# A two-layer graph network on one core: where the output blocks of step 2 get their two layer normalizations

## The chip, the core and the metric

The kernel runs on one core of a Trainium2 chip. The core has five engines with instruction queues of their own: TensorE (PE) for matrix products, VectorE (DVE), ScalarE (ACT), GpSimd (POOL), and SyncE (SP), which here issues most of the DMAs. Each engine works through its queue in order and waits at an instruction until what it needs is there. The metric is the time of one launch on the device, in microseconds; lower is better.

## The reference, cut to what matters

Two layers on 2708 nodes with 256 features. Layer 0 is `x1 = layernorm(x + relu([x, adj @ x] @ W + b))`. Layer 1, on `X = x1`, with `S = adj`:

```
R  = (S + I) / rowsum(S + I)
Xf = Xa = X;  Z = 0
for n in (0, 1):                        # "step 1" and "step 2"
    A  = top_p_attention(Xa)            # softmax, largest entries up to a mass of 0.9, renormalized
    Xf = R @ Xf
    Xa = A @ Xa
    Z  = Z + Xf @ U1[n].T + Xa @ U2[n].T
h   = X + Z
out1 = (h - mean(h)) / sqrt(var(h) + 1e-5) * ln_g + ln_b
out = layernorm(X + out1)
```

The last two lines are what the change is about. For each of the 22 blocks of 128 rows, a block `h` is normalized, multiplied by `g`, added to `x1 + b` (a copy of which lies in HBM as `x1b`), normalized again, and written out.

## The kernel before

All rows are cut into 22 blocks of 128 (the last has 20). Step 2 is a loop over 23 periods (line 1059), and each period over six slots `g` (line 1070). The instructions of all engines are issued in the order in which the Python loop names them; there is no planner, so the order written there is the order in every engine's queue. In period `per`:

- VectorE finds the exact top-p set of block `per`: `last_level` (926 to 930) and `finish2` (934), a generator that is advanced once per slot: line 942 over the whole row, 20 maxima (945), an ordering of 48 candidates (546, 548), small work (955 to 973), five match-replaces (976), of which three come in slot 4 and two in slot 5, and last line 979 over the whole row, which leaves the masked weights.
- TensorE and ScalarE multiply block `per - 1` with `ya`: in each slot `turn` (507) transposes four 128 x 128 pieces on TensorE and ScalarE copies them out of PSUM (516); `products` (522) multiplies the pieces of the slot before. The first transposes of a period need line 979 of the period before.
- ScalarE computes exponentials of block `per + 2` (`exps2`, 785) from logits that TensorE leaves in PSUM, and two trials of a threshold for block `per + 1` (`try_act`, 884, lines 889 and 892 over the whole row). The logits' PSUM tile `lg` is there only once.
- `shift` (781) computes two biases on VectorE: `nmax`, and `half` from it (783).
- `r_units` (687) multiplies gathered columns of `adj` with gathered rows of `yf` or `v`, eight products for each block. GpSimd gathers those rows by indirect DMAs (667), seven for a block, into `yg`, which has room for two blocks; a gather waits until TensorE has used what lay there.
- A block has its `h` when both its product with `R` and its product with the attention weights have arrived (`arrive`, 730, line 737); it is then put in `ready`. `base`, what line 737 adds to, is loaded by SyncE (716).

The finals: `final_slot` (1024) is called once per slot. It takes up to two blocks from `ready` in a period and drives each through its stages in a fixed slot: slot 2 loads `x1b` (996), slot 3 computes mean and variance on VectorE (1001, 1003), slot 4 takes the square root on ScalarE (1008) and then runs `middle` on VectorE (1012 to 1016), which subtracts, multiplies by `g`, scales, adds `x1b`, and computes the second statistics; slot 5 takes the second root; slot 0 of the next period runs `end`, the second normalization on VectorE (145, 146) into a buffer `o`, and the output DMA (1022). `c.gb[:, 0, :]` is `g`.

The buffers: `yg` (477) lies in a room with tag `Y`, used before by the transposed input, and does not fill it. The attention product of step 1 uses the line numbers from 829 to 878; lines 603 (VectorE over the whole row) and 362 (a GpSimd sum of 128 x 128) belong to that step.

Of the kernel before, what the change touches and what calls it, by code (L numbers as in the profile page):

```python
# [133 lines left out]
def ln_stats(nc, small, eps, h, p):  # L134
    st = small.tile([P, 6], FP, tag="bst", name="bst")
    nc.vector.bn_stats(st[:p], h[:p])
    mv = small.tile([P, 2], FP, tag="bmv", name="bmv", bufs=6)
    nc.vector.bn_aggr(mv[:p], st[:p])
    sd = small.tile([P, 1], FP, tag="bsd", name="bsd", bufs=6)
    nc.scalar.activation(sd[:p], mv[:p, 1:2], AF.Sqrt, bias=eps[:p], scale=1.0)  # L140
    return mv, sd
# [7 lines left out]
def fast_path(ctx, tc, c, flags, fint, xT_d, x_d, w0_d, b0_d, w1_d, w2_d, w3_d, u1_d, u2_d, g_d, b_d):  # L149
# [327 lines left out]
    yg = big.tile([P, 2, CC + 1, D], FP, tag="Y", name="yg")  # L477
# [279 lines left out]
    nc.gpsimd.memset(halfn, N / 2)  # L757
    ranks = small.tile([P, 8], FP, tag="ranks", name="ranks", bufs=1)
# [226 lines left out]
    finals = []  # L985

    class Final:
# [10 lines left out]
        def stats(self):  # L998
            p = self.p
            st = small.tile([P, 6], FP, tag="bst", name="bst")  # L1000
            nc.vector.bn_stats(st[:p], self.h[:p])
            self.mv = small.tile([P, 2], FP, tag="bmv", name="bmv", bufs=6)
            nc.vector.bn_aggr(self.mv[:p], st[:p])

        def root(self):
            p = self.p
            self.sd = small.tile([P, 1], FP, tag="bsd", name="bsd", bufs=6)
            nc.scalar.activation(self.sd[:p], self.mv[:p, 1:2], AF.Sqrt, bias=c.eps[:p], scale=1.0)

        def middle(self):  # L1010
            h, p, x1b, sd, mv = self.h, self.p, self.x1, self.sd, self.mv
            nc.vector.reciprocal(sd[:p], sd[:p])
            nc.vector.scalar_tensor_tensor(h[:p], h[:p], mv[:p, 0:1], c.gb[:p, 0, :],
                                           op0=ALU.subtract, op1=ALU.mult)
            nc.vector.scalar_tensor_tensor(h[:p], h[:p], sd[:p], x1b[:p], op0=ALU.mult, op1=ALU.add)
            self.stats()

        def end(self):
            t, p = self.t, self.p
            o = work.tile([P, D], FP, tag="mid", name="o")  # L1020
            ln_apply(nc, o[:p], self.h, p, self.mv, self.sd)
            nc.sync.dma_start(out=out_d[t * P:t * P + p, :], in_=o[:p])

    def final_slot(i):

        if i == 2:
            while ready and len(finals) < 2:
                finals.append(Final(*ready.pop(0)))
        stages = {2: ["load"], 3: ["stats"], 4: ["root", "middle"], 5: ["root"], 0: ["end"]}
        for n in stages.get(i, []):  # L1030
            for f in finals:
                getattr(f, n)()
        if i == 0:
            finals.clear()
# [24 lines left out]
    for per in range(NB + 1):  # L1059
# [10 lines left out]
        for g in range(NG):  # L1070
# [22 lines left out]
            if g == 0:  # L1093
# [4 lines left out]
                final_slot(0)  # L1098
# [11 lines left out]
            if g:  # L1110
                final_slot(g)

# [382 lines left out]
```

## Time and profile before

| what | value |
|---|---|
| time, median of 3 runs | 1440.12 us (1436.54 to 1440.23) |
| span of the profiled run | 1436.7 us |
| TensorE, VectorE, ScalarE, GpSimd busy | 91%, 75%, 51%, 39% |
| step 2's loop over periods | from about 800 us to 1420 us |
| line 1008, table loads for the square root | 8, of 1283 ns |
| line 1013, 1015 on VectorE | 22 each, 466 and 485 ns |
| line 146 on VectorE, into `o` | 22, 412 ns |
| line 362 on GpSimd, 128 x 128 | 22, median 499 ns, longest 3268 ns |
| line 667 on GpSimd, gathers | 308, median 946 ns |

An instruction's row in a timeline gives its start and duration in microseconds, the engine, the line, the operation, what it writes and reads (`out<-in`), the shapes, and in brackets how long the engine sat idle before it and for what. The shares of the first rows are means over stages that have quite different limits: TensorE is busy nearly all of the time in layer 0 and step 1, and less so in the second half of step 2. So the rows for single periods, which the prediction shows, say more about this change.

### The profile page before, as it was taken

How to read it: one execution, taken by the hardware profiler on the slowest of the kernel's cores; microseconds unless marked ns; L12 is line 12 of the kernel's file. 1: busy time of each engine (PE TensorE's matmuls, PEld its weight loads, DVE VectorE, ACT ScalarE, POOL GpSimd, SP SyncE). 2: the span in 40 equal slices, each digit the busy share in tenths (PEclk: the TensorE clock that was granted, in tenths of full speed). 3: DMA queues.
4: the chain of work that ended last, by engine and by line, in shares of the span. 5: the costliest groups of instructions: out<-in, count | busy, mean ns of one | idle time of the engine just before them, and what ended most of it. 6: DMA issues, size and time to landing. Idle time of an engine off the chain costs nothing.

```text
span 1436.7 us, 19034 instructions
## 1 busy us (share of the span) xinstructions
PE 1302.2 (91%) x5788; PEld 913.3 (64%) x5788; DVE 1078.2 (75%) x3665; ACT 729.7 (51%) x1316; POOL 559.1 (39%) x552
## 2 busy tenths in 40 slices
PE   5999999989899999999999699999979887888874
PEld 4778777833566666666664477676657565565652
DVE  1455555865988877777740899999999989898995
ACT  1100001025555555555553588787878776677721
POOL 1000000003454424775552787766247444334410
PEclk8999999999999999999998899999999889788886
DMA  7345444412131110322132546454425433334430
GB/s 205 124 152 159 150 141 148 156 49 68 64 95 64 63 36 20 97 93 69 63 69 66 176 138 189 130 171 127 104 89 163 127 121 121 111 110 132 123 89 24
DMA packets 92832, 157.96 MB, mean 110 GB/s; under 512 B 16356, under 2 KB 65196, under 8 KB 92720
## 3 DMA queue, kind: packets, MB, share of 16 engines
q1 hardware_dynamic: 66434, 100.59, 21.7%
q0 software_dynamic: 20544, 51.17, 12.9%
q10 hardware_dynamic: 5742, 4.89, 1.3%
q8 instruction: 48, 0.79, 0.2%
q14 instruction: 64, 0.52, 0.1%
HBM read 125.33 MB, written 31.26 MB: 109 GB/s over the span
## 4 chain that ended last, share of the span: by engine, by line
PE 54%; DVE 30%; ACT 11%; DMA 2%; issue 2%; SPq 0%; ACTq 0%; DVEq 0%
PE acc L533 16%; PE acc L250 14%; PE lg L493 6%; PE tr L513 5%; DVE e L979 4%; DVE w L976 4%; DVE cand L945 4%; PE misc L646 3%; DVE w L942 3%; ACT w L892 3%; DVE spare L548 2%; ACT w L889 2%; DVE srt L546 2%; PE acc L618 2%; PE misc L420 2%
## 5 line engine op out<-in xcount | busy, mean ns | idle before, releaser
L516 ACT COPY wT<-tr 128x512 f32<-128x512 f32 (+2 forms) x264 | 134.1, 512 | 271.9 <-PE tr L513 269.6
L533 PE MATMUL acc<-ya,wT 128*128 128x256 f32 (+1 forms) x924 | 239.2, 399 | 2.9 <-ACT wT L516 2.9
L667 POOL DMA_INDIRECT yg<-v_d,ix x154 | 153.9, 999 | 197.9 <-PE misc L699 130.8
L533 PE MATMUL acc<-x,wT 128*128 128x256 f32 (+1 forms) x924 | 230.5, 388 | 0.0
L513 PE MATMUL tr<-ident,e 128*128 128x128 f32 (+1 forms) x968 | 160.9, 288 | 73.0 <-DVE bulk L980 70.5
L667 POOL DMA_INDIRECT yg<-yf_d,ix x154 | 181.8, 1181 | 93.0 <-PE misc L699 55.0
L533 PEld LDWEIGHTS acc<-x,wT 128*128 128x128 f32 (+1 forms) x924 | 165.2, 189 | 79.5 <-issue 46.9
L533 PEld LDWEIGHTS acc<-ya,wT 128*128 128x128 f32 (+1 forms) x924 | 175.7, 198 | 56.1 <-issue 22.3
L250 PE MATMUL acc<-y,adj_t 128*128 128x257 f32 (+1 forms) x924 | 208.8, 382 | 0.0
L513 PEld LDWEIGHTS tr<-ident,e 128*128 128x128 f32 (+1 forms) x968 | 121.5, 148 | 123.9 <-issue 97.3
L699 PE MATMUL misc<-yg,adj_t 128*128 128x256 f32 (+1 forms) x660 | 186.3, 418 | 9.1 <-DVE v L722 5.2
L250 PEld LDWEIGHTS acc<-y,adj_t 128*128 128x128 f32 (+1 forms) x924 | 171.5, 189 | 34.0 <-issue 10.3
L360 POOL DMA_INDIRECT adj_t<-in_adj,ix x154 | 169.5, 1101 | 51.0 <-issue 39.3
L699 PEld LDWEIGHTS misc<-yg,adj_t 128*128 128x128 f32 (+1 forms) x660 | 125.1, 204 | 59.0 <-issue 17.7
L493 PE MATMUL lg<-k,q 64*128 64x512 f32 (+3 forms) x528 | 153.5, 610 | 6.7 <-ACT e L789 4.8
L539 DVE MAX8 cand<-e 128x8 f32<-128x170 f32 (+1 forms) x352 | 88.2, 319 | 42.5 <-ACT e L500 42.5
L327 POOL DMA_DIRECT2D part_d<-e x1 | 0.6, 573 | 306.3 <-DVE e L326 306.3
L889 ACT ACTIVATE w<-e,st 128x2708 f32<-128x2708 f32 (+1 forms) x43 | 113.7, 2645 | 0.0
L892 ACT ACTIVATE w<-e,st 128x2708 f32<-128x2708 f32 (+1 forms) x42 | 111.2, 2647 | 0.1
L431 ACT COPY x1T<-tr 128x256 f32<-128x256 f32 (+1 forms) x22 | 8.0, 364 | 192.2 <-PE tr L430 182.8
L945 DVE MAX8 cand<-w 128x8 f32<-128x136 f32 (+1 forms) x440 | 94.4, 285 | 0.8
L546 DVE MAX8 srt<-spare 128x8 f32<-128x128 f32 (+3 forms) x264 | 81.4, 308 | 9.1
(218 smaller groups left out, 1787.5 us busy)
## 6 DMA issues: line engine op xcount, KB each, us to landing
adj_t<-in_adj SPq DMA_DIRECT2D x44, 704.0 KB
adj_t<-adjc_d SPq DMA_DIRECT2D x44, 448.0 KB
adjc_d<-adj_t SPq DMA_DIRECT2D x22, 256.0 KB
base<-za_d SPq DMA_DIRECT2D x41, 128.0 KB
adjc_d<-adj_t SPq DMA_DIRECT2D x22, 192.0 KB
xt<-in_x ACTq DMA_DIRECT2D x21, 128.0 KB
x_d<-x SPq DMA_DIRECT2D x21, 128.0 KB
x1b_d<-xb SPq DMA_DIRECT2D x21, 128.0 KB
```

Of the source, the lines that this page charges most:

```text
L250: nc.tensor.matmul(acc[:p, :n], lhsT=halves[k // KH][:kw, k % KH, :p], rhs=y[:kw, k, :n], start=k == 0, stop=stop and k == NB - 1)
L360: nc.gpsimd.indirect_dma_start(out=a[:CW, i, :], out_offset=None, in_=adj_rows, in_offset=bass.IndirectOffsetOnAxis(ap=ix[:CW, m, i:i + 1] ...
L493: nc.tensor.matmul(lg[:p, h, :b - a], lhsT=q[o, t * P:t * P + p], rhs=keys[s][o, i, :b - a], start=True, stop=True)
L513: nc.tensor.transpose(tr[:kw, k % 4, :p], e[:p, k * P:k * P + kw], ident[:p, :p])
L516: nc.scalar.copy(wT[:, :full, :p], tr[:, :full, :p])
L533: nc.tensor.matmul(acc[:p, :D], lhsT=wT[:kw, k % 4, :p], rhs=y[:kw, k, :], start=k == 0, stop=k == NB - 1)
L546: nc.vector.max(dst[:p, i:i + 8], src[:p])
L667: nc.gpsimd.indirect_dma_start(out=y[:CW, i, :], out_offset=None, in_=rows_d, in_offset=bass.IndirectOffsetOnAxis(ap=ix[:CW, m, i:i + 1], ...
L699: nc.tensor.matmul(acc[:p, :D], lhsT=a[:kw, k, :p], rhs=rhs, start=k == 0, stop=k == CC)
L889: nc.scalar.activation(scr[:b.p, :N], e, AF.Relu, bias=b.nz, scale=b.l[k], accum_out=b.relu)
L892: nc.scalar.activation(scr[:b.p, :N], e, AF.Sign, bias=b.nz, scale=b.l[k], accum_out=b.sign)
L945: nc.vector.max(cand[:p, 8 * i:8 * i + 8], w[:p, SEG2 * i:SEG2 * (i + 1)])
```

## The change

It gives the finals of step 2 another division of labour and another rhythm.

- Normalizing is now `h * (1/sd) + (-mean/sd)`. VectorE computes the two numbers per row (a reciprocal and a product of one column), ScalarE does the 256 columns by an `Identity` activation with a scale and a bias per row. This holds for both normalizations.
- Between them, the product with `g` and the sum with `x1b` go to GpSimd.
- A block's finals are stretched over two periods: in slot 3 it is loaded, in slot 4 first statistics and root, in slot 5 `middle`; in the next period, second statistics and root in slot 4, `end` in slot 5. So in slots 4 and 5 two new blocks (`new`) and two older ones (`finals`) are treated together.
- Since `h` lives longer, the first normalization writes into one of four spare buffers, cut from the unused end of the room with tag `Y`; the second works in place, and the output DMA reads from there. `mv` and `sd` get 8 buffers in place of 6.
- After the last period (`tail`), what is left is done on VectorE as before.
- Apart from that, `half` in `shift` moves from VectorE to ScalarE, between the two exponentials that frame it.

It is meant to take elementwise work from VectorE, and to take the square root out of the middle of VectorE's queue.

```diff
-    yg = big.tile([P, 2, CC + 1, D], FP, tag="Y", name="yg")
+    y_room = big.tile([P, DC * N], FP, tag="Y", name="yg")
+    YW = 2 * (CC + 1) * D
+    yg = y_room[:, :YW].rearrange("p (s c d) -> p s c d", s=2, d=D)
+    spares = [y_room[:, YW + D * i:YW + D * (i + 1)] for i in range(4)]
...
     def shift(b, lg):
         nc.vector.tensor_reduce(b.nmax, lg[:, :P], AX.X, ALU.max, negate=True)
-        nc.vector.tensor_scalar(b.half, b.nmax, 0.5, math.log(F * GUESS ** 0.5), op0=ALU.mult, op1=ALU.add)
...
         if i == 0:
+            nc.scalar.activation(b.half, b.nmax, AF.Identity, bias=part_of[:b.p], scale=0.5)
             nc.scalar.activation(e2(b.t)[:b.p, HC:2 * HC], lg, AF.Exp, bias=b.half, scale=0.5, accum_out=b.roots)
...
+        def norm(self, dst):
+            p, h, mv, sd = self.p, self.h, self.mv, self.sd
+            nc.vector.reciprocal(sd[:p], sd[:p])
+            nc.vector.tensor_scalar(mv[:p, 1:2], mv[:p, 0:1], sd[:p], -1.0, op0=ALU.mult, op1=ALU.mult)
+            if tail:
+                nc.vector.tensor_scalar(h[:p], h[:p], sd[:p], mv[:p, 1:2], op0=ALU.mult, op1=ALU.add)
+            else:
+                nc.scalar.activation(dst[:p], h[:p], AF.Identity, bias=mv[:p, 1:2], scale=sd[:p])
+                self.h = dst
...
         def middle(self):
-            nc.vector.reciprocal(sd[:p], sd[:p])
-            nc.vector.scalar_tensor_tensor(h[:p], h[:p], mv[:p, 0:1], c.gb[:p, 0, :],
-                                           op0=ALU.subtract, op1=ALU.mult)
-            nc.vector.scalar_tensor_tensor(h[:p], h[:p], sd[:p], x1b[:p], op0=ALU.mult, op1=ALU.add)
-            self.stats()
+            if tail:
...
+            spares.append(spares.pop(0))
+            self.norm(spares[-1])
+            h = self.h
+            nc.gpsimd.tensor_tensor(h[:p], h[:p], c.gb[:p, 0, :], op=ALU.mult)
+            nc.gpsimd.tensor_tensor(h[:p], h[:p], self.x1[:p], op=ALU.add)
 
         def end(self):
-            o = work.tile([P, D], FP, tag="mid", name="o")
-            ln_apply(nc, o[:p], self.h, p, self.mv, self.sd)
-            nc.sync.dma_start(out=out_d[t * P:t * P + p, :], in_=o[:p])
+            self.norm(self.h)
+            nc.sync.dma_start(out=out_d[t * P:t * P + p, :], in_=self.h[:p])
 
     def final_slot(i):
-        if i == 2:
-            while ready and len(finals) < 2:
-                finals.append(Final(*ready.pop(0)))
-        stages = {2: ["load"], 3: ["stats"], 4: ["root", "middle"], 5: ["root"], 0: ["end"]}
...
+        if i == 3:
+            while ready and len(new) < 2:
+                new.append(Final(*ready.pop(0)))
+                new[-1].load()
+        if i == 4:
+            for f in new + finals:
+                f.stats()
+            for f in new + finals:
+                f.root()
+        if i == 5:
+            for f in finals:
+                f.end()
+            for f in new:
+                f.middle()
+            finals[:] = new
+            new.clear()
...
-                final_slot(0)
...
+    tail.append(True)
...
-    final_slot(0)
     arrive(t, base, accs.pop(t), ras.pop(t)[:rows(t)])
     while ready or finals:
-        for g in (2, 3, 4, 5, 0):
+        for g in (3, 4, 5):
             final_slot(g)
```

More of the change, by code (lines that the diff above doesn't have):

```diff
@@ L136, in ln_stats @@
     nc.vector.bn_stats(st[:p], h[:p])
-    mv = small.tile([P, 2], FP, tag="bmv", name="bmv", bufs=6)
+    mv = small.tile([P, 2], FP, tag="bmv", name="bmv", bufs=8)
     nc.vector.bn_aggr(mv[:p], st[:p])
-    sd = small.tile([P, 1], FP, tag="bsd", name="bsd", bufs=6)
+    sd = small.tile([P, 1], FP, tag="bsd", name="bsd", bufs=8)
     nc.scalar.activation(sd[:p], mv[:p, 1:2], AF.Sqrt, bias=eps[:p], scale=1.0)
@@ L757, in fast_path @@
     nc.gpsimd.memset(halfn, N / 2)
+    part_of = small.tile([P, 1], FP, tag="part_of", name="part_of", bufs=1)
+    nc.gpsimd.memset(part_of, math.log(F * GUESS ** 0.5))
     ranks = small.tile([P, 8], FP, tag="ranks", name="ranks", bufs=1)
@@ L983, in finish2 @@
         ras[t] = ra
-    finals = []
+    new, finals = [], []
+    tail = []
     class Final:
@@ L1001, in stats @@
             nc.vector.bn_stats(st[:p], self.h[:p])
-            self.mv = small.tile([P, 2], FP, tag="bmv", name="bmv", bufs=6)
+            self.mv = small.tile([P, 2], FP, tag="bmv", name="bmv", bufs=8)
             nc.vector.bn_aggr(self.mv[:p], st[:p])
@@ L1006, in root @@
             p = self.p
-            self.sd = small.tile([P, 1], FP, tag="bsd", name="bsd", bufs=6)
+            self.sd = small.tile([P, 1], FP, tag="bsd", name="bsd", bufs=8)
             nc.scalar.activation(self.sd[:p], self.mv[:p, 1:2], AF.Sqrt, bias=c.eps[:p], scale=1.0)
-        def middle(self):
-            h, p, x1b, sd, mv = self.h, self.p, self.x1, self.sd, self.mv
-            nc.vector.reciprocal(sd[:p], sd[:p])
-            nc.vector.scalar_tensor_tensor(h[:p], h[:p], mv[:p, 0:1], c.gb[:p, 0, :],
-                                           op0=ALU.subtract, op1=ALU.mult)
-            nc.vector.scalar_tensor_tensor(h[:p], h[:p], sd[:p], x1b[:p], op0=ALU.mult, op1=ALU.add)
-            self.stats()
+        def norm(self, dst):
[7 more added lines that the diff above has]
+                self.h = dst
@@ new lines, in middle @@
+        def middle(self):
+            p = self.p
+            if tail:
+                h = self.h
+                mv, sd = self.mv, self.sd
+                nc.vector.reciprocal(sd[:p], sd[:p])
+                nc.vector.scalar_tensor_tensor(h[:p], h[:p], mv[:p, 0:1], c.gb[:p, 0, :],
+                                               op0=ALU.subtract, op1=ALU.mult)
+                nc.vector.scalar_tensor_tensor(h[:p], h[:p], sd[:p], self.x1[:p], op0=ALU.mult, op1=ALU.add)
+                return
+            spares.append(spares.pop(0))
+            self.norm(spares[-1])
+            h = self.h
+            nc.gpsimd.tensor_tensor(h[:p], h[:p], c.gb[:p, 0, :], op=ALU.mult)
+            nc.gpsimd.tensor_tensor(h[:p], h[:p], self.x1[:p], op=ALU.add)
@@ L1029, in final_slot @@
-        stages = {2: ["load"], 3: ["stats"], 4: ["root", "middle"], 5: ["root"], 0: ["end"]}
-        for n in stages.get(i, []):
-            for f in finals:
-                getattr(f, n)()
-        if i == 0:
-            finals.clear()
+        if i == 3:
[7 more added lines that the diff above has]
+                f.root()
```

## The prediction, made before the changed kernel was run

> **What bounds the kernel now.** I first read the slices of the page: in the last third VectorE stands at 9 in almost every slice, TensorE at 7 or 8, so TensorE waits for somebody. The chain of waits then splits the loop over the periods: VectorE rows carry it up to 1075 us, after that ScalarE rows appear between VectorE's. Next, the table by stretch, one period per row (from the end of one line-979 instruction to the end of the next):
>
> ```profile
> 952.30:977.00 24.70, 23.16 (x108) 17.20 (x107) 23.69 (x84) 19.62 (x34) 16.02 (x14) 0.97 0.50 150
> ...
> 1222.40:1254.60 32.20, 27.25 (x110) 19.32 (x110) 28.82 (x103) 23.45 (x38) 13.24 (x14) 0.82 0.40 123
> 1254.60:1286.30 31.70, 26.56 (x110) 19.25 (x110) 29.09 (x102) 23.35 (x38) 13.31 (x14) 0.88 0.41 125
> ```
>
> The columns are length, then busy time of TensorE, weight loads, VectorE, ScalarE, GpSimd, and the clock. A period without finals takes 24.7 us, one with finals 31.8: (1378.26 - 1123.71) / 8 from the starts of line 979. VectorE's busy time rises by 5.3 of those 7 us. The rest is waiting: line 737 waits for `base` (two of eight waits are put down to TensorE) and line 1012 for the square root, in eight periods 8.5 and 3.5 us, so 1.07 and 0.44 per period. The VectorE timeline of 1254.6 to 1286.3 shows both:
>
> ```profile
> 1264.80 0.49 DVE L737 SCALAR_TENSOR_TENSOR h<-acc,ra,base 128x256 f32<-128x256 f32 x1 [0.78 <-DMA base<-za_d]
> ...
> 1278.48 0.16 DVE L1012 RECIPROCAL bsd<-bsd 128x1 f32<-128x1 f32 x1 [0.43 <-ACT bsd L1008]
> 1278.56 0.47 DVE L1013 SCALAR_TENSOR_TENSOR h<-h,bmv,gb 128x256 f32<-128x256 f32 x1
> 1279.06 0.48 DVE L1015 SCALAR_TENSOR_TENSOR h<-h,bsd,x1b 128x256 f32<-128x256 f32 x1
> 1279.58 0.43 DVE L1001 BATCH_NORM_STATS2 bst<-h 128x6 f32<-128x256 f32 x1
> ```
>
> So the loop is bound by VectorE (30.3 us of work and issue), with ScalarE closing a loop beside it: line 979 ends, TensorE transposes, ScalarE works 22.5 us without a pause up to the root (1255.9 to 1278.4), and VectorE cannot get to its last two match-replaces and line 979 before it has that root. TensorE is idle for 5 us per period while it waits for line 979.
>
> **What the Trainium skill says.** (1) "SBUF — State Buffer", section "Who interferes with whom": a VectorE instruction with two SBUF inputs and a GpSimd one that reads SBUF exclude each other; whichever started first keeps the port pair to its end. The trace agrees, both ways:
>
> ```profile
> 462.23 2.13 POOL L362 TENSOR_TENSOR adj_t<-adj_t,ident 128x128 f32<-128x128 f32 x1 [7.84 <-DMA adj_t<-in_adj]
> ...
> 461.02 3.03 DVE L603 SCALAR_TENSOR_TENSOR e<-e,th 128x2708 f32<-128x2708 f32 x1
> 463.98 0.09 DVE L603 DVE_READ_ACCUMULATOR e<-e,th 128x1 f32 x1
> 464.10 0.29 DVE L605 SCALAR_TENSOR_TENSOR flags<-sc 128x1 f32<-128x1 f32 x1
> ```
>
> A GpSimd sum that takes 0.46 to 0.50 us alone takes 2.13 because line 603 runs; and line 605, usually 0.16, takes 0.29 and ends when GpSimd does. (2) "GPSIMD Engine Reference", section "Elementwise — side-by-side cycle accounting": 4497 ns for a sum of 2048 columns. With 0.48 us for 128 columns here, an estimate for 256 columns is 0.48 + 128 x 0.00209 = 0.75 us. (3) "ScalarE: Activation LUTs", section "What ACT_TABLE_LOAD costs": 186 ns + 0.833 ns per element, 93 ns more for each pointer operand, neighbours overlapping by 93 ns. For 256 elements with both operands that gives 0.59 us, 0.50 apart, as an estimate; the trace agrees with its own case, line 889 with both pointers and 2708 elements at 2.645 us (the formula: 2.63).
>
> **The change part by part**, per period with two blocks.
>
> *VectorE's elementwise work.* Removed: lines 1013, 1015 and 146. From start to start, the middle takes 1278.48 to 1281.77 = 3.29 us, less statistics 2 x 0.56 = 2.17; the end 1260.69 to 1261.72 = 1.03; together 3.20. In their place four pairs of a reciprocal and a 1-column product of two scalars. A dependent instruction starts 0.19 to 0.20 after the reciprocal (1260.69 to 1260.88; 1256.53 to 1256.73), the next independent one 0.19 later (1255.21 to 1255.40): 4 x 0.39 = 1.55. Saved: **1.65 us**, all on the path. The statistics stay four per period, moved to the fifth slot.
>
> *`half` on ScalarE.* Line 783 starts 0.31 after line 782 because it needs its result, and the next starts 0.08 later; without it about **0.15 us** less on VectorE, also in the ten periods before the finals (846.85 to 1093.79), which are VectorE's too: 23.69 busy of 24.7, TensorE 23.2. ScalarE gets 0.29 + a gap of about 0.06 (lines 895, 897), with 5 us to spare.
>
> *The root's wait.* The root still sits in the fifth slot on ScalarE, but its reader moves behind line 979. VectorE's 0.44 us disappear. ScalarE may now wait for statistics, but these end on VectorE some 4.6 us before line 979 ends, about 24 us after the preceding one, and ScalarE gets to the roots at about 26.
>
> *The wait for `base`.* SyncE issues in order, and the load of `base` stands behind the two output DMAs, which wait for line 146 (1261.3, 6.7 us after line 979). After: the outputs wait for ScalarE about 2 us after line 979, and `base` has 7 us to land. The 1.07 us go.
>
> *Four normalizations on ScalarE.* They stand between line 979 and the first copy of the next period. First operands at 0.9 (end of search) + 0.4 us after line 979; four at 0.50 spacing end near 3.4, so the first copy starts 2.1 later than now (1.3). Queued behind: table load, exponentials, the logits of slot 1 on TensorE, which need their PSUM tile back. Those start at 6.8 now and would at 7.6: 0.8 us more on TensorE, whose work ends at 26.7 now. ScalarE's chain becomes 3.4 + 22.2 + 0.35 + 1.4 = 27.4. Both remain under VectorE's period below; cost 0.
>
> *Product and sum on GpSimd.* Four at 0.75 = 3.0 us. They start about 3 us after line 979, just where VectorE runs lines 926, 927 and 929 (two SBUF inputs each) and, at 4.1, line 942. Low bound of the loss: 0.1, if VectorE gets in first each time; high bound: 1.9, if all four products and sums (to 6.0) go ahead of line 942. I take one instruction in flight when VectorE needs the port: **0.8 us**.
>
> *Behind them on GpSimd:* 14 gathers of 1.25 us spacing. Those for slots 3 to 5 now follow each TensorE unit that frees their buffer; after, they wait for the sums. If line 942 lies between the two blocks' sums, GpSimd is free at about 9.1; the first gather lands at 12.8 (3.2 us to landing for gathers earlier in this loop), and TensorE needs it at 15.0; the fifth lands at 17.8 for use near 19. In time, by 1 to 2 us. Cost 0, but it makes a rival.
>
> *Buffers.* Four spare buffers last two periods and an output DMA takes a few us; eight `mv` and `sd` likewise: 0.
>
> Sum per full period: 31.82 - 1.07 - 0.44 - 1.65 - 0.15 + 0.8 = **29.3**, a gain of 2.5. Eight of these: 20.0. First period with finals (29.9 us; no ends yet, second statistics gone to the next): 2.17 - 0.78 + 1.12 + 0.57 + 0.15 = 3.2. Last one, with the 20-row block, no line 783 and no waits: 1.65 - 0.5 = 1.1. Ten earlier periods: 1.5. At the end one period's second half is left over, but behind TensorE's edge block; the last block's own chain gets 0.2 for the small product and its statistics stand among others' (1 us), while its `x1b` load is no longer queued behind an output (2.29 us of waiting at 1428.5). I set it to 0. Total 25.8: 1440.1 - 25.8 = **1414**.
>
> **The rivals.**
> - *A, VectorE's work bounds, as above*: with the port's loss from 0.1 to 1.9 us the period is 28.6 to 30.4, and the time 1408 to 1424. For it: the two waits that vanish have releasers that plainly move. Against it: five engines' chains lie within 2 us. Chance 0.72.
> - *B, gathers or late copies hold up TensorE*: if gathers come 3 us late, TensorE's 26.7 + 0.8 + 3 plus its start give a period near 31.0; gain 0.8 x 8 + 5.8 = 12, 1428; at 2 us late about 1423. For it: GpSimd's gathers start at the very end of line 942 in every period, so its port waits are real. Against: two buffers of rows, and idle TensorE time. Chance 0.16.
> - *C, slower*: GpSimd's in-order queue becomes the loop (sums waiting for ScalarE, both long VectorE instructions shutting it out, 17.5 us of gathers, last gathers pushed behind line 979 and then the next sums). At 33.2 us a period that is 8 x 1.4 - 4 = 7 more, 1447. Against: my count for GpSimd is 26.8, or 30.5 with the last gather pushed behind line 979, where it has until about 32. Chance 0.10.
> - *Better than A*: no port loss and a shorter end, under 1405. Chance 0.02.
>
> **How the numbers follow.** Likeliest: A, 1414. 1405 to 1430 holds nearly all of A and most of B, about 0.8. Faster by over 0.3% (under 1435.8): A, most of B, the last: 0.88. Within 0.3%: 0.03. Slower: 0.09, the most of C.
>
> **What would show it.** Starts of line 979 29.3 us apart (28.6 to 30.4) between about 1110 and 1380 us, and 24.55 before the finals; no idle time on VectorE for the root and none for `base`; a gap or a longer small instruction between line 979 and line 942 of about 0.8 us; GpSimd's sums at 0.75 us, or over 3 where line 942 shuts them out; TensorE waiting less than 5 us for line 979, and not for gathers. The prediction is wrong if TensorE's weight loads wait for `yg`, if VectorE waits for ScalarE, or if line 942 starts 2 us or more later after line 979 than the 5.45 us of now plus the four pairs.

## The result, and the profile after

The changed kernel takes **1398.81 us** (median of 4 runs, 1396.17 to 1400.91), beside 1438.33 us for the kernel before on the same chip: ratio **0.9726**, 95% interval 0.9699 to 0.9752. It became faster, as forecast, but the gain is 39.5 us where 25.8 had been added up, and the time lies below the range. On another chip the same two kernels stand the other way round; that is told below, after the experiments on a chip like this one.

Lines after 474 have moved a little: 667 is now 670, 737 is 740, 942 is 947, 979 is 984; 1019 and 1020 are the pairs of small instructions, 1024 ScalarE's normalization, 1040 and 1041 GpSimd's product and sum.

The chain of waits gives the shares by engine in its first line, over the whole span. In the kernel before, VectorE had 30% and ScalarE 11%. In the kernel after:

```profile
PE 54%; DVE 38%; ACT 2%; DMA 2%; issue 2%; SPq 0%; ACTq 0%; DVEq 0%
```

ScalarE has nearly left the chain. In the second half of the loop (1118 to 1369 us) VectorE now carries 74% of it, where before it was VectorE 44% and ScalarE 42% (1124 to 1407 us). In one period, from 1290 to 1324 us, it still runs over ScalarE and TensorE, which deliver just in time. The table by stretch of the kernel after (length, busy time of TensorE, weight loads, VectorE, ScalarE, GpSimd, then clock, DMA share, GB/s), one early period and two full ones:

```profile
972.10:996.60 24.50, 23.18 (x110) 17.08 (x110) 23.52 (x83) 19.93 (x33) 18.64 (x15) 1.00 0.50 150
1233.20:1261.20 28.00, 24.67 (x105) 17.76 (x104) 26.74 (x101) 25.40 (x43) 21.58 (x19) 0.88 0.45 142
1261.20:1289.20 28.00, 25.55 (x122) 18.88 (x121) 26.75 (x101) 25.39 (x43) 21.59 (x19) 1.00 0.46 141
```

A full period is 28.0 us, not 29.3. VectorE is busy for 26.7 of it, and in the list of waits (those over 0.15 us) it has not one entry between 1118 and 1369 us: the other 1.3 us are short gaps between instructions. In the kernel before, period and busy time were some 3 us apart, 1.5 of them waits.

VectorE's timeline in one of these periods; line 984 starts at 1230.18:

```profile
1234.05 0.15 DVE L1019 RECIPROCAL bsd<-bsd 128x1 f32<-128x1 f32 x1
1234.24 0.21 DVE L1020 TENSOR_SCALAR bmv<-bmv,bsd 128x1 f32<-128x1 f32 x1
1234.37 0.15 DVE L1019 RECIPROCAL bsd<-bsd 128x1 f32<-128x1 f32 x1
...
1236.02 0.22 DVE L934 SCALAR_TENSOR_TENSOR st<-st 128x1 f32<-128x1 f32 x1
...
1236.72 3.07 DVE L947 SCALAR_TENSOR_TENSOR w<-e,st 128x2720 f32<-128x2720 f32 x1
...
1242.65 0.47 DVE L740 SCALAR_TENSOR_TENSOR h<-acc,ra,base 128x256 f32<-128x256 f32 x1
...
1258.19 3.05 DVE L984 SCALAR_TENSOR_TENSOR e<-w,st,e 128x2720 f32<-128x2720 f32 x1
```

A pair follows the one before it after 0.32 us (1234.05 to 1234.37). The reciprocal and line 740 have no bracket: nobody waits for a root or for `base`. GpSimd in the same stretch:

```profile
1236.21 0.73 POOL L1040 TENSOR_TENSOR yg<-yg,gb 128x256 f32<-128x256 f32 x1 [2.16 <-ACT yg L1024]
1237.02 3.35 POOL L1041 TENSOR_TENSOR yg<-yg,x1b 128x256 f32<-128x256 f32 x1
1240.33 0.72 POOL L1040 TENSOR_TENSOR yg<-yg,gb 128x256 f32<-128x256 f32 x1
1241.13 0.73 POOL L1041 TENSOR_TENSOR yg<-yg,x1b 128x256 f32<-128x256 f32 x1
```

The first product starts as line 934 ends (1236.24), which needs the port too, and is all but done when line 947 comes (1236.72): line 947 lasts 3.07 instead of the 3.05 it takes without a neighbour. The first sum then loses, and is shut out until line 947 ends. GpSimd pays for the meeting with 2.6 us, which nobody needs; VectorE pays 0.02. So it goes in six of the eight full periods. In the first, line 934 loses 0.55 us and line 947 0.1, in the last line 947 loses 0.2.

Where the profiled spans' 40.6 us (1436.7 to 1396.1) lie, from the starts of line 979 before and line 984 after:

| stretch | before | after | gain | forecast |
|---|---|---|---|---|
| up to the first of these starts, and to the second | 846.85 | 846.32 | 0.5 | 0 |
| ten early periods | 246.94 | 245.16 | 1.8 | 1.5 |
| first period with finals | 29.92 | 26.45 | 3.5 | 3.2 |
| eight full periods | 254.55 | 224.15 | **30.4** | 20.0 |
| last period of the loop | 28.72 | 26.54 | 2.2 | 1.1 |
| behind the last of these starts | 29.72 | 27.48 | 2.2 | 0 |

And one full period by its sections on VectorE (before from 1251.53, after from 1230.18; start to start, in us):

| section | before | after |
|---|---|---|
| line 979 (984) to line 942 (947): small work, pairs | 5.45 | 6.54 |
| line 942 (947) to the ordering: maxima, line 737 (740) | 9.96 | 8.05 |
| ordering to the small work | 5.63 | 4.63 |
| small work | 3.30 | 3.07 |
| three match-replaces | 2.61 | 2.10 |
| middle, or now the four statistics | 3.29 | 2.13 |
| last two match-replaces | 1.48 | 1.49 |

### The profile page after: what moved, and what is told of

Its sections match the earlier page's. It is cut to its first block, busy times and chain, and to the rows that moved or that the text cites. A ratio compares the mean times of both kernels' runs of the same rounds, so it can differ in the third digit from the quotient of the medians.

```text
span 1396.1 us, 19129 instructions
## 1 busy us (share of the span) xinstructions
PE 1287.6 (92%) x5788; PEld 903.6 (65%) x5788; DVE 1054.3 (76%) x3624; ACT 757.1 (54%) x1381; POOL 645.5 (46%) x595
## 4 chain that ended last, share of the span: by engine, by line
PE 54%; DVE 38%; ACT 2%; DMA 2%; issue 2%; SPq 0%; ACTq 0%; DVEq 0%
PE acc L536 16%; PE acc L250 15%; PE lg L496 6%; DVE cand L950 6%; DVE w L981 5%; DVE e L984 5%; DVE w L947 4%; PE tr L516 4%; PE misc L649 3%; DVE spare L551 3%; DVE srt L549 3%; PE acc L621 2%; PE misc L420 2%; PE acc L452 2%; PE misc L415 2%
## 5 line engine op out<-in xcount | busy, mean ns | idle before, releaser
L670 POOL DMA_INDIRECT yg<-yf_d,ix x154 | 196.6, 1276 | 80.6 <-PE misc L702 43.7
L670 POOL DMA_INDIRECT yg<-v_d,ix x154 | 169.8, 1103 | 77.6 <-DMA v_d<-v 32.4
L250 PEld LDWEIGHTS acc<-y,adj_t 128*128 128x128 f32 (+1 forms) x924 | 171.5, 189 | 34.0 <-issue 10.3
L702 PE MATMUL misc<-yg,adj_t 128*128 128x256 f32 (+1 forms) x660 | 175.1, 397 | 12.8 <-DVE v L725 5.2
L516 PE MATMUL tr<-ident,e 128*128 128x128 f32 (+1 forms) x968 | 153.1, 278 | 16.8 <-DVE bulk L985 14.2
L516 PEld LDWEIGHTS tr<-ident,e 128*128 128x128 f32 (+1 forms) x968 | 117.4, 142 | 64.3 <-issue 30.2
L702 PEld LDWEIGHTS misc<-yg,adj_t 128*128 128x128 f32 (+1 forms) x660 | 117.4, 192 | 62.0 <-issue 18.2
```

The lines of the kernel that those rows point to most:

```text
L250: nc.tensor.matmul(acc[:p, :n], lhsT=halves[k // KH][:kw, k % KH, :p], rhs=y[:kw, k, :n], start=k == 0, stop=stop and k == NB - 1)
L516: nc.tensor.transpose(tr[:kw, k % 4, :p], e[:p, k * P:k * P + kw], ident[:p, :p])
L670: nc.gpsimd.indirect_dma_start(out=y[:CW, i, :], out_offset=None, in_=rows_d, in_offset=bass.IndirectOffsetOnAxis(ap=ix[:CW, m, i:i + 1], ...
L702: nc.tensor.matmul(acc[:p, :D], lhsT=a[:kw, k, :p], rhs=rhs, start=k == 0, stop=k == CC)
```

## The experiments on the chip where the change gains

These four ran on one chip, where the kernel before took 1435.44 us (15 runs). Whether the pair above ran on this same chip is not on record; the kernel before differs by 0.2% between the two, and both are called the first chip below.

**The rhythm alone: `rhythm_dve`.** The new order of stages, but all elementwise work of the finals on VectorE; `half` stays on ScalarE.

```diff
-    tail = []
+    tail = [True]
```

> The changed kernel in its new rhythm (finals over two periods, roots in slot 4, outputs in slot 5), but with all elementwise work of the finals on VectorE: 'tail' is set from the start. Theory: a full period of the changed kernel is nothing but VectorE's queue, so the work comes back and no wait does. Middle: reciprocal and two 256-column instructions, about 1.10 a block in place of 0.32; end: about 0.72 in place of 0.32; 2.4 us a period, so line-984 starts 30.4 us apart and about 1420 us; no idle time for base or root. Rival (the rhythm itself is worth nothing, all came from the moved work): 31.8 apart, 1436 to 1440.

Measured: 1421.14 us, ratio 0.9906 (0.9886 to 0.9926). Line 984 starts 30.3 us apart on average. VectorE's waits between 1120 and 1360 us (us in total, times, longest) have shrunk to one line, where the kernel before has 12 us of them between 1123 and 1380:

```profile
DVE h L740 <- PE tr L516: 1.1, 1, 1.1
```

So the rhythm removes the waits for `base` and the root by itself, and with `half` brings the period from 31.8 to 30.3 us; the division of labour brings the rest (30.3 to 28.0). Both mechanisms of the forecast are there, at their places.

**Nothing on GpSimd: `no_pool`.** Product and sum are left out inside the loop, so this kernel computes less.

```diff
-            nc.gpsimd.tensor_tensor(h[:p], h[:p], c.gb[:p, 0, :], op=ALU.mult)
-            nc.gpsimd.tensor_tensor(h[:p], h[:p], self.x1[:p], op=ALU.add)
```

> The changed kernel without GpSimd's product with g and sum with x1b in the loop (left out; the tail keeps them). Theory (GpSimd's work costs the full periods nothing): starts of line 984 still 28.0 apart, only the first period with finals up to 1 us shorter, 1397 to 1399. Rival (GpSimd's sums cost something hidden, through late gathers and the port): 0.5 us a period or more, 1394 or less.

Measured: 1397.07 us, ratio 0.9736 (0.9712 to 0.9759), starts 27.9 us apart. The interval holds the changed kernel's ratio. The port, which the forecast charged with 0.8 us a period, costs about 0.1.

**The product ahead of line 947's neighbours: `middle_first`.** The new blocks are normalized before the older ones, so that GpSimd starts two normalizations earlier.

```diff
-            for f in finals:
-                f.end()
             for f in new:
                 f.middle()
+            for f in finals:
+                f.end()
```

> The changed kernel with the two loops of slot 5 exchanged: the new blocks' middle before the older blocks' end. The first GpSimd product then starts about 1.0 us earlier after line 984 ends (2.0 in place of 3.05), while VectorE still has to run lines 931, 932, 934 and 947. Theory (the port loss that I had put at 0.8 us was avoided only by where the first product happens to fall, between 934 and 947): now 931 or 934 and then 947 wait for GpSimd, 0.7 to 1.5 us a period, 1405 to 1411. Rival (GpSimd's short instructions never cost VectorE anything): 1399, within 0.3%.

Measured: 1402.16 us, ratio 0.9774 (0.9753 to 0.9795), starts 28.4 apart: 0.4 more. VectorE's timeline shows who pays now, and GpSimd's for what:

```profile
1236.64 0.39 DVE L931 SCALAR_TENSOR_TENSOR st<-st 128x1 f32<-128x1 f32 x1
...
1237.31 0.52 DVE L934 SCALAR_TENSOR_TENSOR st<-st 128x1 f32<-128x1 f32 x1
1238.32 3.05 DVE L947 SCALAR_TENSOR_TENSOR w<-e,st 128x2720 f32<-128x2720 f32 x1
```

```profile
1236.28 0.73 POOL L1040 TENSOR_TENSOR yg<-yg,gb 128x256 f32<-128x256 f32 x1 [5.36 <-ACT yg L1024]
1237.09 0.73 POOL L1041 TENSOR_TENSOR yg<-yg,x1b 128x256 f32<-128x256 f32 x1
1237.78 0.72 POOL L1040 TENSOR_TENSOR yg<-yg,gb 128x256 f32<-128x256 f32 x1
1238.58 3.37 POOL L1041 TENSOR_TENSOR yg<-yg,x1b 128x256 f32<-128x256 f32 x1
```

Lines 931 and 934 (0.21 and 0.22 us in the changed kernel) end when GpSimd's instructions do, but between two of GpSimd's instructions VectorE gets in. The first product and the first sum cost 0.2 + 0.3 us; the second sum is shut out by line 947 again. So the loss exists, and here each time it is no more than the rest of one short instruction; the high end of 1.9 us supposed that GpSimd keeps the port through a whole series.

**One wait alone: `base_first`.** The kernel *before*, with the load of `base` issued ahead of the two outputs.

```diff
-                final_slot(0)
                 if per > 1:
 ...
                     later.append(lambda t=t, base=base: arrive(t, base, accs.pop(t), ras.pop(t)[:rows(t)]))
+                final_slot(0)
```

> The kernel before with one exchange in slot 0: the load of base is put ahead of the call that issues the two outputs, so that it no longer waits behind them. Theory 1 (waits add up, as in my forecast): the 1.07 us a period for base go, 30.75 us a period, about 1430. Theory 2 (two loops side by side, of which the one through ScalarE's root is 31.7 us long by itself): VectorE merely gets to the root earlier and waits there, root waits rise from 0.44 to about 1.3 us, the period stays 31.6 to 31.8, 1437 to 1440.

Measured: 1433.87 us, ratio 0.9989 (0.9978 to 1.0000). VectorE's waits between 1123 and 1380 us, first the kernel before, then this one:

```profile
DVE h L737 <- DMA base<-za_d: 6.5, 6, 2.0
DVE bsd L1012 <- ACT bsd L1008: 3.5, 6, 1.2
```

```profile
DVE bsd L1012 <- ACT bsd L1008: 11.0, 7, 1.9
```

The wait for `base` is gone, and the wait for the root has grown by about as much; the first seven full periods are 31.8 us long on average, where the kernel before has 31.9. Only the eighth is shorter, 29.8 in place of 31.3, about what the run gains (1.6 us). ScalarE's chain from one line 979 to the root ran *beside* VectorE and was no shorter. The two waits were one limit, seen at two places, and subtracting either alone would have been a mistake; the change removes both, which is why the forecast's sum of the two held.

## The same change on other chips

Then three groups of runs fell on two chips where the kernel before takes 1466 to 1468 us, and one on a third where it takes 1471.7. The first group was to undo the change in parts.

**`half` back on VectorE: `half_back`.**

```diff
         nc.vector.tensor_reduce(b.nmax, lg[:, :P], AX.X, ALU.max, negate=True)
+        nc.vector.tensor_scalar(b.half, b.nmax, 0.5, math.log(F * GUESS ** 0.5), op0=ALU.mult, op1=ALU.add)
 ...
-            nc.scalar.activation(b.half, b.nmax, AF.Identity, bias=part_of[:b.p], scale=0.5)
```

> The changed kernel with half computed on VectorE again, as before, and not on ScalarE. Theory: every period with a block b_exp is VectorE's, so each of about 19 gets 0.18 to 0.20 us longer: 24.7 apart before the finals, 28.2 with them, 3.5 to 4 us in all against the changed kernel, 1402 to 1403. Rival (ScalarE's extra instruction delays the exponentials by as much, so the move is worth nothing): the same as the changed kernel within 0.1%, 1398 to 1399.

**The old rhythm with the new division of labour: `old_rhythm`.** Normalizations on ScalarE and product and sum on GpSimd, but both halves of the finals within one period, as before.

```diff
+            spares.append(spares.pop(0))
+            self.norm(spares[-1])
 ...
+            nc.gpsimd.tensor_tensor(h[:p], h[:p], c.gb[:p, 0, :], op=ALU.mult)
+            nc.gpsimd.tensor_tensor(h[:p], h[:p], self.x1[:p], op=ALU.add)
 ...
-        stages = {2: ["load"], 3: ["stats"], 4: ["root", "middle"], 5: ["root"], 0: ["end"]}
+        stages = {2: ["load"], 3: ["stats"], 4: ["root", "middle", "stats"], 5: ["root"], 0: ["end"]}
```

> The kernel before with only the new division of labour: both normalizations on ScalarE into the spare buffers, product and sum on GpSimd, but all stages in the slots of before (root and middle in slot 4 with the second statistics right after, end in slot 0, half on VectorE). Theory (the stretching over two periods is what makes the new engines usable): VectorE's second statistics wait in its queue for root, ScalarE 0.6, GpSimd 0.73 + 0.73, about 3 us a period, while 2.6 us of VectorE's work are gone; period 31.5 to 33, 1436 to 1450. Rival (what counts is the work taken from VectorE): about 30, 1415 to 1422.

**Four pairs as one: `batched`.** The changed kernel with one root, one reciprocal and one product on four columns.

```diff
-            nc.vector.reciprocal(sd[:p], sd[:p])
-            nc.vector.tensor_scalar(mv[:p, 1:2], mv[:p, 0:1], sd[:p], -1.0, op0=ALU.mult, op1=ALU.mult)
 ...
+                nc.vector.reciprocal(sd4[:, :n], sd4[:, :n])
+                nc.vector.scalar_tensor_tensor(mv4[:, :n, 1], mv4[:, :n, 0], -1.0, sd4[:, :n],
+                                               op0=ALU.mult, op1=ALU.mult)
```

> The changed kernel with the four blocks' statistics in one tile of four columns: one square root, one reciprocal and one product of four columns in place of four each. Theory (VectorE's queue is all there is in a full period): four pairs took 1.28 us, one pair about 0.35, so 0.9 less a period, 27.1 apart, 8 us in all, 1390 to 1392. Rival (another loop is already as long: ScalarE through its copies and the logits, or GpSimd's gathers behind its sums): under 0.4 a period, 1396 to 1399.

**More for GpSimd: `pool_more`.** Two further products with `g` ahead of the right ones. In this case `g` is all ones, so the output stays the same.

```diff
+            nc.gpsimd.tensor_tensor(h[:p], h[:p], c.gb[:p, 0, :], op=ALU.mult)
+            nc.gpsimd.tensor_tensor(h[:p], h[:p], c.gb[:p, 0, :], op=ALU.mult)
```

> The changed kernel with three products with g for each block in place of one (g is all ones, so the values stay): 4 x 0.73 = 2.9 us more on GpSimd per period. Theory (GpSimd is nearly full: its last gathers of a period already run into line 984): GpSimd's queue becomes the loop and TensorE waits for gathers, 0.8 to 1.5 us a period more, 1406 to 1412. Rival (GpSimd has room, its gathers have a whole half period of lead): 28.0 as now, 1399 to 1400.

Measured, beside 1466.24 us: `half_back` 1489.2, 1.0158 (1.0130 to 1.0187); `old_rhythm` 1495.0, 1.0196 (1.0163 to 1.0228); `batched` 1478.29, 1.0088 (1.0059 to 1.0117); `pool_more` 1474.62, 1.0053 (1.0026 to 1.0081). All are slower than the kernel before, so the question became whether the changed kernel itself is. (What these four were meant to show on the first chip, the worth of `half`, of the rhythm by itself, of the pairs and of GpSimd's room, stays untested there.)

> The changed kernel unaltered, as a reference for the runs beside it: in the runs of half_back, old_rhythm, batched and pool_more the kernel before took 1466 us where it had taken 1435 to 1440, and VectorE waited up to 3.8 us at a time for nothing that the profile names ('remote', 'issue'). Theory (these waits come from the chip or its neighbours): here line 984 starts 28.0 us apart, ratio to before 0.972 to 0.976. Rival (the changed kernel itself has two speeds): ratio near 1 or above, with the same unnamed waits.

> As for batched: the four blocks' root, reciprocal and product once for all. Theory (VectorE's queue is all there is in a full period): 27.1 apart, 8 us less than the changed kernel beside it. Rival (another loop is already as long): under 0.4 a period, under 4 us.

> As for old_rhythm: new division of labour in the slots of before. Theory (only the stretching makes it usable): VectorE waits about 2.8 us a period for GpSimd's sums, base as late as before, slower than the kernel before by 5 to 15 us. Rival (the work taken from VectorE counts): 15 to 25 us faster than before.

> As for pool_more: three products for each block on GpSimd in place of one, 2.9 us more per period. Theory (GpSimd is nearly full): TensorE waits for gathers, 0.8 to 1.5 us a period more, 8 to 13 us more than the changed kernel beside it. Rival (room and lead enough): the same within 2 us.

Measured, beside 1467.98 us: **the changed kernel 1489.49, ratio 1.0150** (1.0101 to 1.0198); `batched` 1481.15, 1.0099 (1.0063 to 1.0135); `old_rhythm` 1497.49, 1.0210 (1.0178 to 1.0242); `pool_more` 1470.65, 1.0018 (1.0005 to 1.0030). The kernel that gains 2.7% on one chip loses 1.5% on this one.

`old_rhythm` is explained by waits with names. Between 1120 and 1380 us VectorE waits, on the chip with 1466.24,

```profile
DVE h L740 <- DMA base<-za_d: 25.6, 7, 4.7
DVE bst L1004 <- POOL yg L1018: 19.6, 14, 2.0
```

so the chain from VectorE to ScalarE to GpSimd and back does not fit into one period, whose length is 35.2 to 36.0 us: without the new rhythm the division of labour brings back more waits than it removes work. That this holds on the first chip too is argued from these waits; `old_rhythm` did not run there.

The others show something else: engines that stand still without a releaser (the trace calls it "remote", an unknown queue, or "issue"). Here is ScalarE in the changed kernel on the chip with 1467.98, with the transposes on TensorE that its copy waits for, then GpSimd at that time:

```profile
1208.61 0.19 ACT L894 ACTIVATION_READ_ACCUMULATOR w<-e,st 128x1 f32 x1
...
1210.06 0.60 PE L516 MATMUL tr<-ident,e 128*128 128x128 f32 x4
...
1218.47 0.58 ACT L519 COPY wT<-tr 128x512 f32<-128x512 f32 x1 [9.67 <-remote]
```

```profile
1198.70 0.99 POOL L670 DMA_INDIRECT yg<-v_d,ix  x1
1199.99 0.95 POOL L670 DMA_INDIRECT yg<-v_d,ix  x1 [0.30 <-issue]
...
1215.00 0.95 POOL L670 DMA_INDIRECT yg<-v_d,ix  x1 [0.30 <-issue]
```

GpSimd issues 14 gathers without a pause, one each 1.25 us, from 1198.70 to 1215.95; ScalarE stops 10 us into this row and goes on 2.5 us after it. What it waits for is old by then: the transposes end at 1210.66. VectorE stands still in this row too, between two instructions of its own, of which the second needs only the first:

```profile
1212.10 0.42 DVE L1007 BATCH_NORM_STATS2 bst<-h 128x6 f32<-128x256 f32 x1
1215.64 0.18 DVE L1009 BATCH_NORM_AGGREGATE bmv<-bst 128x2 f32<-128x6 f32 x1 [3.13 <-remote]
```

On the first chip 0.03 us lie between these two. The trace also records when the signal comes by which an instruction tells that it has ended. Line 1007 ends at 1212.52 and its signal comes at 1215.62; the transposes end at 1210.66 and theirs comes at 1218.44. Each time the waiting engine goes on within 0.03 us of the signal. On the first chip VectorE's signals come within 0.1 us of the end. So in a stop the work is done, and the signal is late. All eleven stops of VectorE in this trace between 1100 and 1400 us are waits for a signal of VectorE itself. That no releaser is named follows from this, and from gaps in the traces of these chips: of VectorE's 2006 signals this one holds 1562, where the first chip's holds all.

GpSimd's sums bring such rows about: by the time they are done, TensorE has freed the buffers of all 14 gathers, which in the kernel before were issued in twos and threes as TensorE went along. What draws the stops was tried with the kernel before and two parts left out:

> The kernel before, unaltered, for its trace on the same chip as the three kernels beside it. If the chip behaves like the first one (about 1437 us), the trace repeats the one shown: line 979 starts 31.8 us apart, and VectorE, ScalarE and TensorE have no waits without a named releaser to speak of. If it behaves like the later two chips (about 1467 us), I expect its last periods to be longer than 31.8 us too, with idle time that no releaser explains, but less of it than the changed kernel shows there (periods of 33 to 35 us); if it has none, such waits come from what the change adds.

> The changed kernel with GpSimd's product and sum left out inside the loop. On a chip like the first it gave 0.9736, as the changed kernel does. On a chip like the later two, where the changed kernel needs 1.015 times the time of the kernel before: if the sums push the gathers into a dense row at the end of the period and that brings the waits without a name, leaving them out gives 1.00 or less; if the waits come from the new rhythm or from ScalarE's instructions, it stays at 1.01 to 1.02.

> The new rhythm (second half of the finals a period later) with all elementwise work on VectorE as before; half on ScalarE stays. On a chip like the first it gave 0.9906. On a chip like the later two: if what is dense on GpSimd or ScalarE brings the waits without a name, 0.99 to 1.00 again; if the rhythm itself does (statistics of four blocks in slot 4), 1.01 to 1.02.

> The changed kernel with the four pairs of a reciprocal and a one-column product (1.28 us measured in one period) replaced by one pair on four columns, and the four square roots by one on four columns. Theory (VectorE's own work bounds the full periods): on a chip like the first, 1.28 - 0.32 = 0.96 less in the nine full periods, 8 to 9 us less than 1398.8, so about 1390, ratio near 0.967 against the kernel before, with line 979's starts 27.1 apart. Rival (another engine is by now level with VectorE): periods stay at 27.8 to 28.0, 1397 to 1399. On a chip like the later two it was 0.5% faster than the changed kernel, and should be near 1.01 again.

Measured, beside 1465.68 us (the same chip as the changed kernel's second run): the kernel before 1464.36 in its one run; `no_pool` 1425.86, **0.9721** (0.9705 to 0.9738); `rhythm_dve` 1451.25, **0.9888** (0.9868 to 0.9907); `batched` 1482.97, 1.0093 (1.0061 to 1.0126). Without product and sum on GpSimd, the ratios are those of the first chip (0.9736 and 0.9906). So all that the change costs there, 1.015 against 0.972, about 63 us, hangs on GpSimd's product and sum being where they are.

The kernel before gave the control, with the row of 14 gathers that it has where the loop goes over from `yf` to `v`. GpSimd, then ScalarE:

```profile
1076.98 0.94 POOL L667 DMA_INDIRECT yg<-v_d,ix  x1 [32.77 <-PE tr L513]
...
1093.24 0.95 POOL L667 DMA_INDIRECT yg<-v_d,ix  x1 [0.30 <-issue]
```

```profile
1087.83 0.19 ACT L905 ACTIVATE st<-st 128x1 f32<-128x1 f32 x1
1092.61 0.58 ACT L516 COPY wT<-tr 128x512 f32<-128x512 f32 x1 [4.60 <-remote]
```

Here too ScalarE stops 11 us into the row, and this one period has 30.4 us where its neighbours have 24.7; afterwards the full periods are 31.8 us long, as on the first chip. Set instruction against instruction, this trace falls 26 us behind the first chip's: about 6 at this row, 12 at a row of 21 gathers (816 to 842 us) and 3 at one of 11 (757 to 771 us), and the rest in small steps earlier. ScalarE stops at the row of 11 too and VectorE at that of 21. On the first chip no engine stops at the row of 11, and the 21 are broken up by gathers drawn out to 2.7 us and more. So most of what makes the kernel before slower on this chip lies at rows as well. If the rows and not the sums are to blame, it is enough to put the sums elsewhere in GpSimd's queue:

**The sums later: `sums_slot3` and `sums_slot2`.** The changed kernel with product and sum issued in slot 3 or slot 2 of the next period, behind all 14 gathers or behind the first 7.

```diff
+            self.late = True
 ...
+        def rest(self):
+            if not self.late:
+                return
+            self.late = False
 ...
             nc.gpsimd.tensor_tensor(h[:p], h[:p], c.gb[:p, 0, :], op=ALU.mult)
             nc.gpsimd.tensor_tensor(h[:p], h[:p], self.x1[:p], op=ALU.add)
 ...
     def final_slot(i):
 ...
+        if i == 3:
+            for f in finals:
+                f.rest()
         if i == 3:
```

In `sums_slot2` the new condition is `if i in (2, 3)`; `late` sees to it that each block gets them once.

> The changed kernel with GpSimd's product and sum issued in slot 3 of the next period, behind the gathers that TensorE's slots 0 to 2 free, in place of at once. Where the changed kernel is slow (before about 1466 us): theory (14 gathers in one dense row of 17.5 us, which the sums bring about, draw the waits without a name): the row is broken up, these waits go, line 984 starts about 28 us apart again, 1425 to 1435, ratio 0.972 to 0.98; the sums may make VectorE wait up to 1 us a period for the second statistics. Rival (GpSimd's product and sum themselves bring the waits, or the work they add to GpSimd's queue in any order): 1.01 to 1.02 as before. Where it is fast (before about 1437 us): 1397 to 1406, ratio 0.972 to 0.978, since no port is lost there and only the wait for the second statistics can be new.

> As sums_slot3, but product and sum in slot 2: behind the 7 gathers freed by slots 3 to 5 and ahead of the 7 freed by slots 0 to 2, so these 7 pile up behind the sums and the others don't. Where the changed kernel is slow: if the length of the dense row decides, waits without a name become shorter but some may stay, 1425 to 1460; with the rival 1.01 to 1.02. Where it is fast: as the changed kernel, 1397 to 1402, ratio 0.972 to 0.975; the second product or sum is shut out by line 947 once a period, as there.

Measured, beside 1471.7 us on a fourth chip: `sums_slot3` 1440.33, **0.9780** (0.9755 to 0.9806); `sums_slot2` 1441.33, **0.9789** (0.9763 to 0.9815). They compute all that the changed kernel computes, and beat the kernel before on a chip of the slower kind. (The changed kernel itself did not run on this one.) GpSimd in `sums_slot2`:

```profile
1249.99 0.73 POOL L1050 TENSOR_TENSOR yg<-yg,x1b 128x256 f32<-128x256 f32 x1
1250.87 0.99 POOL L670 DMA_INDIRECT yg<-v_d,ix  x1
...
1258.42 0.95 POOL L670 DMA_INDIRECT yg<-v_d,ix  x1 [0.30 <-issue]
1261.39 0.95 POOL L670 DMA_INDIRECT yg<-v_d,ix  x1 [2.02 <-PE misc L702]
```

The row now has 7 gathers, the eighth waits for TensorE again, and no engine stops. Counted over the stretch from 1100 to 1400 us in each trace (a row: gathers of which each starts less than 1.4 us after the one before, so that one drawn out by VectorE ends it; stops: waits of over 1.5 us without a releaser on ScalarE and VectorE together):

| kernel, time of the kernel before on its chip | rows of 10 to 14 | stops, us |
|---|---|---|
| before, 1440 and 1466 | 0 | 0 |
| changed, 1438 | 9 | 0 |
| `middle_first`, 1435 | 9 | 0 |
| changed, 1468 | 8 | 21, 90.4 |
| `batched`, 1468 | 8 | 20, 87.9 |
| `half_back`, 1466 | 8 | 19, 73.1 |
| `pool_more`, 1468 | 8 | 16, 69.4 |
| `old_rhythm`, 1468 (seven rows of 8) | 0 | 0 |
| `no_pool`, 1466 (one row of 8) | 0 | 0 |
| `rhythm_dve`, 1466 | 0 | 2, 10.3 |
| `sums_slot3`, 1472 | 0 | 1, 5.6 |
| `sums_slot2`, 1472 | 1 | 2, 14.0 |

The stops of the last three, like those of the kernel before, end within 4 us of the end of the row near 1080 to 1104 us, which every kernel has on these chips. So on these chips, and not on the first, rows of ten or more stop the other engines, from about the tenth microsecond of the row on; three rows of 12 or 13 did not, one in `sums_slot2` and one in each of the two traces of `pool_more`. The bound was set after the counting, and what makes a row was too: by the pauses alone (0.30 us) the gathers of `old_rhythm` stand in rows of 14 as well, but two in each are drawn out to 2.6 and 3.3 us while VectorE runs a long instruction, and nothing stops. So it is 10 us and more of gathers at 1.25 us each that goes with the stops; no run varied this spacing by itself. (TensorE is left out of the count: in `sums_slot3` four of its eight waits for the logits' tile, 2 to 4 us each, carry no releaser, where the other four name ScalarE.) `pool_more` is faster than the changed kernel there although its GpSimd has more to do; its rows come some 3 us later in the period, but why that helps was not tried.

**What stays open** is why the signals come late in a row, and what differs between the chips. Whether the recording of the traces, which has gaps on just these chips, has a share in it is not shown either: as far as the record tells, no run was made without it. An obvious thought was that instructions come late. The Trainium skill, "Runtime: NRT & Kernel Launch", section "Instruction fetch mechanics", says that an engine's sequencer fetches its instructions in blocks of 16 KiB by a DMA queue of its own. The profile agrees for one queue: `q8 instruction` moved 48 packets with 0.79 MB in the changed kernel. The other, `q14 instruction`, moved 63 with 0.52 MB, half as much each. But on the slow chip no packet of either instruction queue falls between 1191 and 1220 us, ahead of the stop at 1208.6, in it, or at its end; and the DMA engines are busy at about a third while it lasts. So these traces don't show it, and speak against it.

## Why the prediction was right in direction and wrong in size

By its own steps, on the chip where both kernels were measured first:

- **The bound** was named rightly: VectorE. After the change it is so more than before (26.7 of 28.0 us busy, no waits), though the chain by ScalarE and TensorE is close behind; how close was not measured. Rival C did not come about on this chip. B neither: TensorE's wait for the attention weights (line 980, now 985) fell from 70.5 us to 14.2 us in all. Its weight loads did wait for gathered rows, which had been named as a sign of being wrong, but only 4 times and 3.1 us in all in the full periods (before: once, 0.8 us), and no wait of VectorE stands behind them.
- **The waits for `base` and the root**, 1.07 + 0.44: right as a sum. That one alone would have brought nothing (`base_first`) had been said in half, by "a loop beside it", but was not used to test the sum.
- **VectorE's elementwise work**: removed 3.20 is right (3.27 by the sections above); in its place 4 x 0.39 was put, and 4 x 0.32 measured. The second instruction of a pair and the next reciprocal overlap: 1234.24 to 1234.37 is 0.13, where 0.19 was taken from other neighbours. 0.27 a period.
- **`half`**: 0.20 where 0.15 was set; in the ten early periods 1.8 in all where 1.5 was.
- **The port's loss is the step that failed.** 0.8 us a period was taken, from bounds of 0.1 and 1.9, by supposing that one instruction of GpSimd is in flight when VectorE wants the port. In the changed kernel 0.02 is lost in most periods and 0.12 on average, without GpSimd's part 0.1 is gained, and with the sums put in VectorE's way 0.4 to 0.5 is lost. This one term is 5.4 of the 10.4 us that the eight periods missed; the pairs and `half` are 2.6, and 2.4 have no name. Part of it could have been known: the first product (3.0 to 3.75 us after line 979) meets a short instruction at most. Line 942 was put at 4.1, where its own parts give 3.8 (2.4 now, plus 1.55, less 0.15; 3.5 was measured), and at 3.8 it comes just ahead of the first sum, as it did.
- **The end, set to 0**, brought 2.2. The forecast had seen the likely cause (2.29 us of waiting at 1428.5 for a load behind an output; that wait is gone), and set it against costs of about 1 us that were not worked out. The last period brought 2.2 where 1.1 was set, the start of the loop 0.5.
- **Costs set to 0 that cost VectorE nothing**: ScalarE's four normalizations (TensorE does wait for the logits' tile, 24 us in the full periods, with room for it), the gathers, the buffers.

What was missed adds up: 10.4 + 2.2 + 1.1 + 0.3 + 0.3 + 0.5 = 14.8 = 40.6 - 25.8. Even with the port at its low bound the sum was 1408; all the smaller terms erred to the same side. "Better than A" had been written down with its two causes, no port loss and a shorter end, and with a chance of 0.02.

On the other chips something decides that no step had contained, the late signals. Rival C named the place, GpSimd's queue with its gathers pushed together, but by another way: the queue is not what the others wait for, and GpSimd itself waits for ScalarE ahead of its sums (12.0 us in the period shown).

## What to carry to other kernels

When a step has bounds as wide as 0.1 to 1.9 us, ask in the timeline whether the two instructions would really meet, and who would be first, before taking a middle; and add up terms that were rounded to nothing, since they need not cancel. Waits of two chains that run beside each other count once: taking one away only moves the time to the other. Work that is put in front of an in-order queue changes the spacing of all that stands behind it; look at what was spread out and becomes a row, and place the new work where the queue waits anyway. And when a wait names no releaser, compare the end of the work that it needs with the signal of that end.

## What the runs showed of the hardware that was not expected

A GpSimd instruction seems to give up the port somewhat before its recorded end: line 947 starts at 1236.72, the product's record ends at 1236.94, and line 947 takes 3.07 where it takes 3.05 alone. Or the record ends late by some 0.2 us; the trace does not tell these apart. The Trainium skill, "SBUF — State Buffer", section "Who interferes with whom", speaks of an exclusive lock; between GpSimd's instructions VectorE got in each time (lines 931 and 934 with `middle_first`). And on three of the chips, in a row of ten or more gathers on GpSimd, VectorE and ScalarE stand still for 1.6 to 10 us at a time, and TensorE behind them, although the work that they wait for is done: the signal comes late, even from VectorE to itself. On the first chip rows of 14 did nothing of the sort. The time of one kernel on one chip, and even the sign of a change, need not carry over to the next chip.
